# Attention and a symmetrised 7 x 7 depthwise convolution: the convolution on VectorE by even and odd parts of its kernel

## The chip, the cores and the metric

One core of a Trainium2 chip runs the whole program. The metric is the device time of one execution in microseconds (us). PE is TensorE's matmul unit, PEld its weight load, DVE is VectorE, ACT is ScalarE, POOL is GpSimd and SP is SyncE, which here only issues DMAs. Line numbers such as L524 are those of the kernel before.

## What is computed

The input x is (16, 384, 32, 32) in float32. Two residual layers follow each other, each on a group norm without affine terms (32 groups of 12 channels):

```python
x = x + attention(gn(x), w_qkv, w_proj, b_proj)   # 8 heads of 48, 1024 tokens
w_sym = (w + rot90(w, 1) + rot90(w, 2) + rot90(w, 3)) * 0.25
x = x + depthwise_conv(gn(x), w_sym, padding=3)   # 384 channels, 7 x 7
```

w_sym is unchanged by a rotation of 90 degrees, so it is also unchanged by one of 180: w_sym[dy, dx] = w_sym[-dy, -dx].

## The kernel before

**Tiles.** An image is three tiles of 128 channels by 1024 tokens (NK = 3). The 16 images go one after the other through the attention; the second norm and the convolution of image b run beside the attention of image b + 1.

**TensorE** per image: q and k for all heads (qk_step, L445), v (v_step, L471), then 64 pairs of steps: s_step (L516) makes scores of 1024 columns in PSUM, ScalarE takes their exponential (L524), av_step (L536) multiplies by v. The PSUM pool ps_s has 3 buffers, so a score step waits for the exponential of three steps before. A pair of heads ends with take (L549), sums_out (L556, L560: the softmax sums travel by SP's DMA queue), invert (L566 reciprocal, L568 and L571 the inverses out and back over SP's queue) and divide (L578). project (proj_step, L597, L605) adds the projection to x by an accumulating DMA on POOL's queue (L612). The projection of the last image is done in parts (L627, L641).

**The second norm** of image b: means on VectorE (x1_means, L1099), three squares with sums on ScalarE (x1_squares, L288), the sums gathered over groups by two DMAs on POOL's queue (ch_x L294, gs_x L296), bn_aggr (L300), then groups_x1: Ln and Exp on ScalarE (L306, L307, with two table loads), a product (L308), and spread: gr_x (L277) and sc_x (L281), two small DMAs on POOL's queue that bring scale and offset to the channels. x1_chains then has ScalarE make the normalised tiles xn (L367), one per channel tile. Image 14 takes groups_x1_vector instead, with 1/sigma on VectorE, and its x1_chains is due at once.

**The convolution.** Three of the 48 tiles run on TensorE at the very end: (14, 2), (15, 2), (15, 1), written (image, tile). Their normalised rows are stored by SP (conv_store, L758), loaded in shifted form as sh (conv_load, L765, four DMAs for a quarter of a tile), and multiplied by diagonal matrices (conv_on_pe, L799), 14 taps per half, or 13 for (14, 2). The other 45 tiles run on VectorE: conv_tap (L683) multiplies a shifted view of xn by a weight and adds it to x, once for each of 49 taps; the three tiles of an image take turns. Of (14, 0), (15, 0) and (14, 2) the seven or three taps with dx = 0 are ScalarE products (product, L664) that POOL's queue adds (add_rows, L997); (15, 0) has two sums that are added at the end (L970, L976, stores L977).

The statistics of the first norm are taken for images 2 to 15 at the start (xs, L383, L390). A general version of the whole program follows under a condition that these inputs don't meet (run(True)); it is not executed.

**The order of the work** is written out by a planner in Python, ahead of the run. clock follows TensorE, vclock VectorE. catch_up fills VectorE: what after() put into the heap later and is due comes first, then tap(), the next convolution pass. Work for ScalarE waits in applies, first in first out, with a due time and a cost; act_slot puts it between the exponentials where the cost fits a slot (3.0 us at a v step, 4.3 us between steps). Each engine and each DMA queue issues in the order that results, and an instruction that waits holds up everything behind it on its engine or queue. qk_rest issues six DMAs on POOL's queue (L461) for the q and k of an image, and begin_x the three loads of the next image's x (L164, 512 KB each). loads(1) issues one quarter of sh; in the last image it is called at the steps r = 32, 40 and 48 and at the start of the last projection.

Of the kernel before, what the change touches and what calls it, by code (L numbers as in the profile page):

```python
# [45 lines left out]
def kernel(  # L46
# [51 lines left out]
    wc = consts.tile([P, NK, KS, KS], F32, name="wc")  # L98
    nc.gpsimd.dma_start(
# [11 lines left out]

    def run(general):
        tag = "g" if general else "f"
        with ExitStack() as stack:
# [9 lines left out]
            npool = pool("npool", 6)  # L124
            qkpool = pool("qkpool", 5)
# [18 lines left out]
            LONE = (B - 1, 0)  # L144

            ROWS_ONLY = {PE_TILES[0]: (1, 2, 3), LONE: range(-PAD, PAD + 1)}

            BESIDE = None if general else (B - 2, 0)
            ROWS_ONLY[BESIDE] = range(-PAD, PAD + 1)

            def taps_of(b, k):
                return [t for t in TAPS if t[1] or t[0] not in ROWS_ONLY.get((b, k), ())]
# [49 lines left out]
            eye = wpool.tile([P, P // 4], F32, name="eye")  # L202
            wsh = wpool.tile([P, 2, 4, 2, KS], F32, name="wsh")
# [32 lines left out]
            class Stats:  # L236
# [65 lines left out]
                def groups_x1(self):  # L302

                    af = small.tile([GROUPS, 2], F32, tag="af", name=f"af_{self.name}")
                    ln = small.tile([GROUPS, 1], F32, tag="ln", name=f"ln_{self.name}")
                    nc.scalar.activation(ln, self.mv[:, 1:2], AF.Ln, bias=eps[0:GROUPS])  # L306
                    nc.scalar.activation(af[:, 0:1], ln, AF.Exp, scale=-0.5)  # L307
                    nc.scalar.activation(  # L308
                        af[:, 1:2], self.mv[:, 0:1], AF.Identity, scale=af[:, 0:1]
                    )  # L310
                    self.spread(af)

# [66 lines left out]
            def stream_in(b, k):  # L379
                if not many:  # L380
                    many["bs"] = npool.tile([P, B - 2, NK, 12], F32, tag="xn1", name="bs_all")
                many[b, k] = rpool.tile([P, N], F32, tag="x1", name=f"xs_{b}_{k}")
                nc.gpsimd.dma_start(  # L383
                    many[b, k], x[b, k * P : (k + 1) * P].rearrange("p h w -> p (h w)")
                )
# [12 lines left out]
            def stream_gather():  # L398
# [9 lines left out]
                gs = npool.tile([P, 4, PER * 12], F32, tag="xn1", name="gs_all")  # L408
# [247 lines left out]
            spare = {}  # L656

            def new_xn1(b, k):
                return npool.tile([P, N], F32, tag="xn1", name=f"xn1_{b}_{k}")

            def product(dst, b, k, dy):

                rows, src = ((slice(i.start * W, i.stop * W)) for i in region(dy)[0])
                nc.scalar.activation(  # L664
                    dst[:, rows],
                    xn1s[b, k][:, src],
                    AF.Identity,
                    scale=wsym[:, k, dy + PAD, PAD : PAD + 1],
                )
                return dst[:, rows], rows  # L670

# [3 lines left out]
            def conv_begin(st, b, k, engine):  # L675
                xn1s[b, k] = spare.pop((b, k), None) or new_xn1(b, k)
                st.apply(xn1s[b, k], x1s[b, k], k, engine)

            def conv_tap(b, k, dy, dx, dst=None):
                (oy, iy), (ox, ix) = region(dy, dx)  # L680
                dst = x1s[b, k] if dst is None else dst
                acc = dst.rearrange("p (h w) -> p h w", w=W)[:, oy, ox]
                nc.vector.scalar_tensor_tensor(  # L683
                    acc,
                    xn1s[b, k].rearrange("p (h w) -> p h w", w=W)[:, iy, ix],
                    wsym[:, k, dy + PAD, dx + PAD : dx + PAD + 1],
                    acc,
                    ALU.mult,
                    ALU.add,
                )  # L690
# [88 lines left out]
            def pe_taps(b, k):  # L779
                return [t for t in PE_TAPS if t != (1, 0) or (b, k) not in ROWS_ONLY]  # L780

            def conv_on_pe(b, k, h, first, last):
# [9 lines left out]
                taps = pe_taps(b, k)  # L792
# [120 lines left out]
            clock, vclock, last_image, catching = 0.0, 0.0, 1e9, False  # L913
            later, count = [], 0
            chains, active = deque(), []
# [14 lines left out]
            def us_tap(dy, dx):  # L930
                late_us = 0.02 if clock > last_image else 0.0
                return ((H - abs(dy)) * (W - abs(dx)) + (128 if active else 268)) / 955 + late_us

            def tap():

                while len(active) < NK and chains:
                    active.append([*chains.popleft(), 0])
                if not active:
                    return 0.0
                b, k, n = active[0]  # L940
                if (b, k) == LONE:
                    active.append(active.pop(0))
                    return tap_of_two(b, k, active[-1])
                taps = taps_of(b, k)
                c = active.pop(0)
                c[2] += 1
                if n < len(taps):
                    took = us_tap(*taps[n])
                    conv_tap(b, k, *taps[n])
                else:  # L950
                    assert not applies
                    took = us_tap(0, 0)
                    nc.vector.tensor_tensor(x1s[b, k], x1s[b, k], late["beside"], ALU.add)
                if c[2] < len(taps) + ((b, k) == BESIDE):
                    active.append(c)
                else:
                    conv_end(b, k)
                return took

            def tap_of_two(b, k, c):  # L960

                n = c[2]
                c[2] += 1
                taps = taps_of(b, k)
                if n < len(taps):
                    conv_tap(b, k, *taps[n], late["sum2"] if n % 2 else None)
                elif n == len(taps):
                    assert not adds
                    dst = late["sum2"]
                    nc.vector.tensor_tensor(dst, dst, late["sum3"], ALU.add)  # L970
                else:

                    for h in range(2):
                        cols = slice(h * HALF, (h + 1) * HALF)
                        dst = x1s[b, k][:, cols]
                        nc.vector.tensor_tensor(dst, dst, late["sum2"][:, cols], ALU.add)  # L976
                        (nc.sync, nc.scalar)[h].dma_start(  # L977
                            out[b, k * P : (k + 1) * P].rearrange("p h w -> p (h w)")[:, cols], dst
                        )
                    active.remove(c)  # L980
                return (950 + 128) / 955


            adds = deque()

            def add_step(due):
                nonlocal count
                add_rows(*adds.popleft())
                if adds:
                    due += 8.0  # L990
                    count += 1
                    heapq.heappush(later, (due, count, 0.0, lambda: add_step(due)))

            def add_rows(b, k, t, rows):
                dst = {LONE: late.get("sum3"), BESIDE: late.get("beside")}.get((b, k))
                dst = dst if dst is not None else x1s[b, k]
                nc.gpsimd.dma_start(dst[:, rows], t, accum_op=ALU.add)  # L997

            def rows_early(b, k, n, dy):
                if (b, k) == BESIDE and dy == 0:  # L1000
                    product(late["beside"], b, k, dy)
                    return

                t, rows = product(spare[B - 1, 1 + n % 2], b, k, dy)
                add_rows(b, k, t, rows)

            def lone_sums(b, k):

                product(late["sum2"], b, k, 0)
                product(late["sum3"], b, k, 1)  # L1010

            def lone_rows(b, k):

                for dy in (-1, 2, -2, 3, -3):
                    e = epool.tile([P, 2, HALF], F32, tag="e", name=f"tap_{dy}")
                    adds.append((b, k, *product(flat(e), b, k, dy)))
                add_step(now())
# [28 lines left out]
            def issue(c):  # L1046
# [15 lines left out]
                else:  # L1062
                    act_slot(3.0)
# [4 lines left out]

            applies = deque()
            ON_VECTOR = ()  # L1070

            def project(b):
                nonlocal clock
                for o in range(NK):
                    proj_step(b, o)
                    clock += US_PROJ
                    if b in ON_VECTOR:
                        after(8.0, 1.3, lambda o=o: x1_part(b, o))
                if b not in ON_VECTOR:
                    after(1.6, 0.2, lambda: x1_means(b))  # L1080

            def x1_part(b, k):

                if k == 0:
                    x1_stats[b] = Stats(f"x1_{b}")
                st = x1_stats[b]
                st.channels(x1s[b, k], k)
                if k == NK - 1:
# [431 lines left out]
```

## Time and profile before

| | us |
|---|---|
| median of 3 runs | 2910.88 (2908.89 to 2915.01) |
| the profiled execution | 2910.56 |
| its span | 2908.8 |
| mean granted TensorE clock | 0.991 of full speed |
| VectorE in L683, 2170 taps | 2362.5 |
| ScalarE in L524, 1024 exponentials | 1020.4 |
| TensorE in L516 and L536 | 1037.8 and 1036.8 |

The span runs from the first to the last record of the profiled execution; the execution's own time lies 1.76 us above it. A share of busy time is a mean over the span. In a timeline, a row gives the start, the time, the engine and line, the operation, its output and inputs, how many instructions were joined in the row, and in brackets how long the engine sat idle before it and what ended that. A list of waits gives, for an engine and line, what it waited for, the total, the number of times and the longest. A row of windows gives busy time and instruction count for PE, PEld, DVE, ACT and POOL in turn, then the granted clock, the busy share of the DMA engines and GB/s.

### The profile page before, as it was taken

Reading aid. Unit: us, or ns where it says so; the run is one execution under the profiler, and the core shown is the slowest. Engines: PE = TensorE matmul, PEld = TensorE weight load, DVE = VectorE, ACT = ScalarE, POOL = GpSimd, SP = SyncE. Lnnn points to the kernel's source line nnn. Section 1 sums busy time; section 2 is a strip of 40 time slices with the busy share of each in tenths; the row PEclk is TensorE's granted clock in tenths of the full one; section 3 lists DMA queues with packets and bytes.
Section 4 is the critical chain, followed back from the end, with each engine's and each line's share of the span. In section 5 each row is a group of like instructions: output and inputs, shape, how many; then the busy total and the mean of one; then the engine's idle time right before and its main releaser. Section 6 shows DMA issues by size and latency. Waiting matters only on the chain. (4 is left out here: it accounts for less than half of the span.)

```text
span 2908.8 us, 46868 instructions
## 1 busy us (share of the span) xinstructions
PE 2860.4 (98%) x19638; PEld 1137.1 (39%) x19638; DVE 2570.7 (88%) x2562; ACT 1573.6 (54%) x1873; POOL 252.2 (9%) x411
## 2 busy tenths in 40 slices
PE   9999999999999999999999999999999999998986
PEld 5343343433434343443434334343443434343332
DVE  4502999999999999999999999999999999999679
ACT  3637556374754737466473745637375473744720
POOL 3200012000101001010100101000010100101100
PEclk9999999999999999999999999999999999999998
DMA  6621121121302122121212212122131212212625
GB/s 239 184 44 41 28 57 50 38 70 25 81 20 65 38 43 63 29 70 33 65 38 42 64 29 55 46 42 64 29 77 27 58 39 42 64 29 43 154 58 149
DMA packets 77485, 176.86 MB, mean 61 GB/s; under 512 B 32096, under 2 KB 34032, under 8 KB 75728
## 3 DMA queue, kind: packets, MB, share of 16 engines
q0 software_dynamic: 34336, 114.90, 15.6%
q1 hardware_dynamic: 41216, 55.21, 7.3%
q10 hardware_dynamic: 1712, 3.67, 0.4%
q8 instruction: 156, 2.56, 0.4%
q14 instruction: 65, 0.53, 0.1%
HBM read 118.61 MB, written 28.72 MB: 51 GB/s over the span
## 5 line engine op out<-in xcount | busy, mean ns | idle before, releaser
L683 DVE SCALAR_TENSOR_TENSOR x<-xn,wsym,x 128x930 f32<-128x930 f32 (+9 forms) x2170 | 2362.5, 1162 | 14.7 <-ACT xn L367 14.7
L524 ACT ACTIVATE e<-ps_s 128x1024 f32<-128x1024 f32 x1024 | 1020.4, 1029 | 484.0 <-PE ps_s L516 483.4
L516 PE MATMUL ps_s<-qk 48*64 48x512 f32 x8192 | 1037.8, 590 | 11.7 <-ACT e L524 11.7
L536 PE MATMUL acc<-e,v 64*64 64x512 f32 x8192 | 1036.8, 590 | 0.0
L516 PEld LDWEIGHTS ps_s<-qk 48*64 48x64 f32 x8192 | 309.0, 133 | 588.4 <-issue 534.6
L536 PEld LDWEIGHTS acc<-e,v 64*64 64x64 f32 x8192 | 311.4, 133 | 571.7 <-issue 570.8
L445 PE MATMUL ps_qk<-x,wqk 128*128 128x512 f32 x1152 | 502.4, 595 | 0.0
L445 PEld LDWEIGHTS ps_qk<-x,wqk 128*128 128x128 f32 x1152 | 218.1, 190 | 277.7 <-issue 269.3
L452 ACT COPY qk<-ps_qk 128x1024 f32<-128x1024 f32 x96 | 97.2, 1013 | 333.9 <-PE ps_qk L445 333.5
L471 PE MATMUL ps_v<-wv,x 128*128 128x384 f32 x768 | 252.6, 486 | 0.0
L597 PE MATMUL ps_proj<-o,wp 128*128 128x512 f32 x540 | 234.2, 592 | 0.0
L491 ACT COPY v<-ps_v 64x384 f32<-64x384 f32 x256 | 121.6, 475 | 150.8 <-PE ps_v L471 148.5
L471 PEld LDWEIGHTS ps_v<-wv,x 128*128 128x128 f32 x768 | 145.9, 190 | 108.2 <-issue 14.4
L612 POOL DMA_DIRECT2D x<-in_x x45 | 39.3, 874 | 1610.8 <-ACT x L605 1439.0
L597 PEld LDWEIGHTS ps_proj<-o,wp 128*128 128x128 f32 x540 | 102.6, 190 | 126.2 <-issue 122.2
L566 DVE RECIPROCAL rec<-sums 128x16 f32<-128x16 f32 x63 | 15.6, 248 | 152.2 <-DMA sums<-sum 152.2
L605 ACT ACTIVATE x<-ps_proj,bp 128x1024 f32<-128x1024 f32 x45 | 50.2, 1115 | 167.5 <-PE ps_proj L597 167.5
L578 DVE TENSOR_TENSOR o<-o,inv 128x1024 f32<-128x1024 f32 x63 | 76.8, 1218 | 48.2 <-DMA inv<-inv 36.4
L549 ACT COPY o<-acc 128x512 f32<-128x512 f32 x128 | 68.5, 591 | 72.0 <-PE acc L536 72.0
L390 DVE BATCH_NORM_STATS2 bs_all<-xs 128x6 f32<-128x512 f32 x84 | 52.7, 681 | 39.6 <-DMA xs<-in_x 39.5
L799 PE MATMUL ps_conv<-sh,mat 128*32 128x480 f32 (+3 forms) x656 | 68.0, 569 | 0.0
L367 ACT ACTIVATE xn<-x,sc_x 128x1024 f32<-128x1024 f32 x47 | 55.3, 1271 | 11.6 <-DVE sc_x L357 7.2
(144 smaller groups left out, 594.8 us busy)
## 6 DMA issues: line engine op xcount, KB each, us to landing
x<-in_x POOLq DMA_DIRECT2D x90, 512.0 KB, 5.6
inv<-inv SPq DMA_DIRECT2D x126, 256.0 KB
out<-x POOLq DMA_DIRECT2D x45, 512.0 KB, 3.7
xs<-in_x POOLq DMA_DIRECT2D x42, 512.0 KB, 6.9
qk<-qk POOLq DMA_DIRECT2D x96, 128.0 KB, 4.2
o<-o SPq DMA_DIRECT2D x180, 32.0 KB
sh<-xd SPq DMA_DIRECT2D x32, 160.0 KB
x<-in_x SPq DMA_DIRECT2D x6, 512.0 KB
```

The source lines that it names most:

```text
L445: nc.tensor.matmul(ps[:, h, :], lhsT=wqk[:, k, s, t, :], rhs=xns[b][:, k, h * HALF : (h + 1) * HALF], start=(k == 0), stop=(k == NK - 1),)
L452: nc.scalar.copy(halves(qks[u][:, s, :]), ps)
L471: nc.tensor.matmul(ps[:, j, 0:C], lhsT=xns[b][:, k, t * P : (t + 1) * P], rhs=wv[:, k, :], start=(k == 0), stop=(k == NK - 1),)
L491: nc.scalar.copy(dst[:, :, 0 : HEADS // 2 * (D + 1)].rearrange("p k (h d) -> p k h d", d=D + 1)[:, :, :, 0:D], src.rearrange("p k (h d) -> ...
L516: nc.tensor.matmul(ps[64 * c : 64 * c + 64, a, :], lhsT=qk[r, 1, 64 * kb : 64 * kb + 64], rhs=qk[r, 0, h * HALF : (h + 1) * HALF], start=True,
L524: nc.scalar.activation(es[n], ps, AF.Exp, scale=SCALE)
L536: nc.tensor.matmul(accs[a][64 * j : 64 * j + 64, :], lhsT=v[rows, kb, c : c + 64], rhs=e[rows, j, :], start=(kb == 0), stop=(kb == 2 * NT ...
L549: nc.scalar.copy(half_of(w)[:, a, :], accs.pop(a))
L578: nc.vector.tensor_tensor(o, o, invs.pop(u).rearrange("p (a n) -> p a n", a=2), ALU.mult)
L597: nc.tensor.matmul(ps[:, h, :], lhsT=wp[:, t, o * P : (o + 1) * P], rhs=os_[b, t // 2][:, t % 2, h * HALF : (h + 1) * HALF], start=(t == 0 ...
L683: nc.vector.scalar_tensor_tensor(acc, xn1s[b, k].rearrange("p (h w) -> p h w", w=W)[:, iy, ix], wsym[:, k, dy + PAD, dx + PAD : dx + PAD + 1],
L799: nc.tensor.matmul(dst[CH * i : CH * (i + 1), :].rearrange("p (y x) -> p y x", x=W)[:, :, ox], lhsT=mats[k][:, i, d0 * KS + dx + PAD, :], ...
```

## The change

**The passes.** With w_sym[dy, dx] = w_sym[-dy, -dx], the kernel is split by dx: even(dy, dx) is half the sum and odd(dy, dx) half the difference of w_sym at dx and -dx (four more small VectorE operations at the start; odd vanishes for dx = 0 and for dy = 0). For each tile ScalarE writes the normalised rows into a padded tile with a pitch of 35 (fold_x) and makes the three products with even(dy, 0), dy = 1 to 3 (fold_first). VectorE makes three sums and three differences of the view shifted by +dx and -dx (side), builds three rows of sums with even and three with odd weights, and adds each to the output shifted by +dy and by -dy, with the sign turned for the odd ones. That makes 34 passes and three products by tensor_scalar for each tile instead of 49 taps, one tile at a time.

**ScalarE** no longer makes products of single tap rows (L664, with L970, L976 and L997), and Ln and Exp of the second norm are gone: all images take groups_x1_vector. The three squares of the norm may stand at a v step, since the slot there is 4.3 instead of 3.0. applies becomes a heap by due time. x1_chains of every image is due 9 us after the statistics, that of image 14 too. prepare decides when fold_x and fold_first of a tile are put into applies.

**Order and buffers.** On POOL's queue gr_x and sc_x of an image stand directly behind the three loads of L164; ch_x and gs_x stand before the six DMAs of L461. npool has named tiles in one buffer instead of six rotating ones, qkpool 4 buffers instead of 5; the matrix tile mat_1 lies in the space of wqk and the masks in that of wv. loads(1) is called at r = 32 and 40 only. All three TensorE tiles have 14 taps per half. The last tile on VectorE is (15, 0), whose last addition is cut in two halves with a store each.

```diff
+        near, far = wsym[:, :, PAD:, PAD:], wsym[:, :, PAD:, PAD::-1]
+        nc.vector.tensor_tensor(even, near, far, ALU.add)
+        nc.vector.tensor_scalar(even, even, 0.5, None, ALU.mult)
+        nc.vector.tensor_tensor(odd, near, far, ALU.subtract)
+        nc.vector.tensor_scalar(odd, odd, 0.5, None, ALU.mult)
...
-            npool = pool("npool", 6)
-            qkpool = pool("qkpool", 5)
+            npool = pool("npool", 6 if general else 1)
+            qkpool = pool("qkpool", 4)
...
-            LONE = (B - 1, 0)
-
-            ROWS_ONLY = {PE_TILES[0]: (1, 2, 3), LONE: range(-PAD, PAD + 1)}
-
-            BESIDE = None if general else (B - 2, 0)
-            ROWS_ONLY[BESIDE] = range(-PAD, PAD + 1)
-
-            def taps_of(b, k):
-                return [t for t in TAPS if t[1] or t[0] not in ROWS_ONLY.get((b, k), ())]
+            LAST = (B - 1, 0)
...
+                padded = [
+                    npool.tile([P, H * PITCH + 2 * PAD], F32, name=f"padded_{i}") for i in range(2)
+                ]
+                for t in padded:
+                    nc.gpsimd.memset(t, 0.0)
+                sides = [npool.tile([P, N], F32, name=f"side_{j}") for j in range(PAD)]
+                rows_e = [npool.tile([P, N], F32, name=f"rows_e{i}") for i in range(PAD)]
...
-                def groups_x1(self):
-
-                    af = small.tile([GROUPS, 2], F32, tag="af", name=f"af_{self.name}")
-                    ln = small.tile([GROUPS, 1], F32, tag="ln", name=f"ln_{self.name}")
-                    nc.scalar.activation(ln, self.mv[:, 1:2], AF.Ln, bias=eps[0:GROUPS])
-                    nc.scalar.activation(af[:, 0:1], ln, AF.Exp, scale=-0.5)
-                    nc.scalar.activation(
-                        af[:, 1:2], self.mv[:, 0:1], AF.Identity, scale=af[:, 0:1]
-                    )
-                    self.spread(af)
...
+            def padded_view(i, d=0):
+
+                return padded[i % 2][:, PAD + d : PAD + d + H * PITCH].rearrange(
+                    "p (h w) -> p h w", w=PITCH
+                )[:, :, 0:W]
+
+            def fold_x(i, st, b, k):
+                nc.scalar.activation(
+                    padded_view(i),
+                    grid(x1s[b, k]),
+                    AF.Identity,
+                    bias=st.sc[:, k, 1:2],
+                    scale=st.sc[:, k, 0:1],
+                )
+
+            def fold_first(i, k):
+
+                for dy in range(1, PAD + 1):
+                    nc.scalar.activation(
+                        grid(rows_e[dy - 1]),
+                        padded_view(i),
+                        AF.Identity,
+                        scale=even[:, k, dy, 0:1],
+                    )
...
+                def side(j, n, op):
+                    vec.tensor_tensor(grid(sides[n]), padded_view(i, j), padded_view(i, -j), op)
+
+                def into(dst, src, w):
+                    vec.scalar_tensor_tensor(dst, src, w, dst, ALU.mult, ALU.add)
+
+                def first(dst, src, w):
+                    vec.tensor_scalar(dst, src, w, None, ALU.mult)
+
+                def shifted(src, dy, op, half=None):
+                    lo, hi = max(0, -dy) * W, (H - max(0, dy)) * W
+                    if half is not None:
+                        lo, hi = (lo, N // 2) if half == 0 else (N // 2, hi)
+                    dst = out_t[:, lo:hi]
+                    vec.tensor_tensor(dst, dst, src[:, lo + dy * W : hi + dy * W], op)
...
+                for j in (1, 2, 3):
+                    sums.append((full, lambda j=j: side(j, j - 1, ALU.add)))
+                outs.append((full, lambda: into(grid(out_t), padded_view(i), e(0, 0))))
+                for j in (1, 2, 3):
+                    outs.append((full, lambda j=j: into(out_t, sides[j - 1], e(0, j))))
+
+                def out_rows(t, dy, second):
+                    part = ((H - dy) * W + 128) / 955
+                    outs.append((part, lambda: shifted(t(), dy, ALU.add)))
+                    outs.append((part, lambda: shifted(t(), -dy, second)))
+
+                for dy in (1, 2, 3):
+                    for j in (1, 2, 3):
+                        sums.append(
+                            (full, lambda dy=dy, j=j: into(rows_e[dy - 1], sides[j - 1], e(dy, j)))
+                        )
+                    out_rows(lambda dy=dy: rows_e[dy - 1], dy, ALU.add)
+                for n, j in enumerate((2, 3, 1)):
+                    sums.append((full, lambda j=j, n=n: side(j, n, ALU.subtract)))
+                slot = {2: 0, 3: 1, 1: 2}
+                for n, (dy, (j, l)) in enumerate(((1, (2, 3)), (2, (3, 1)), (3, (1, 2)))):
+                    sums.append(
+                        (ts, lambda dy=dy, j=j, n=n: first(rows_o[n % 2], sides[slot[j]], o(dy, j)))
+                    )
+                    sums.append(
+                        (full, lambda dy=dy, l=l, n=n: into(rows_o[n % 2], sides[slot[l]], o(dy, l)))
+                    )
+                    out_rows(lambda n=n: rows_o[n % 2], dy, ALU.subtract)
...
+            applies, count_a = [], 0
+
+            def add_apply(when, cost, f):
+
+                nonlocal count_a
+                count_a += 1
+                heapq.heappush(applies, (when, count_a, cost, f))
...
+            def prepare():
+
+                n = state["x"]
+                if n < len(order) and n < state["done"] + 2:
+                    state["x"] += 1
+                    add_apply(now() + (1.0 if n > state["done"] else 0.0), 1.3, lambda n=n: prepare_x(n))
+                n = state["rows"]
+                if n < len(order) and n <= state["free"] and n in ready_x:
+                    state["rows"] += 1
+                    add_apply(now() + (2.5 if n > state["done"] else 0.0), 3.6, lambda n=n: prepare_rows(n))
+
+            def prepare_x(n):
+                b, k, st = order[n]
+                fold_x(n, st, b, k)
+                ready_x[n] = now() + 2.0
+                prepare()
+
+            def prepare_rows(n):
+                fold_first(n, order[n][1])
+                ready_rows[n] = now() + 4.0
+                prepare()
...
-                    act_slot(3.0)
+                    act_slot(4.3)
...
-                after(11.0, 3.3 if b == B - 2 else 0.6, lambda: x1_aggregate(b, st))
+                after(11.0, 3.3, lambda: x1_aggregate(b, st))
 
             def x1_aggregate(b, st):
                 st.aggregate()
-                if b == B - 2:
-
-                    st.groups_x1_vector()
-                    applies.append((now(), 3.7, lambda: x1_chains(b, st)))
-                else:
-                    applies.append((now() + 0.5, 0.6, lambda: x1_groups(b, st)))
-
-            def x1_groups(b, st):
-                st.groups_x1()
-                applies.append((clock + 9.0, 3.7, lambda: x1_chains(b, st)))
+                st.groups_x1_vector()
+                add_apply(now() + 9.0, 1.3, lambda: x1_chains(b, st))
...
+                order.extend((b, k, st) for k in range(NK) if (b, k) not in on_pe)
+                prepare()
...
-                if b == B - 1 and r in (32, 40, 48):
+                if b == B - 1 and r in (32, 40):
```

## Prediction

> **What bounds the kernel now.** I read the busy shares first, then what TensorE waited for, then each wait's neighbourhood in the timelines, then the end. The page:
>
> ```profile
> span 2908.8 us, 46868 instructions
> ## 1 busy us (share of the span) xinstructions
> PE 2860.4 (98%) x19638; PEld 1137.1 (39%) x19638; DVE 2570.7 (88%) x2562; ACT 1573.6 (54%) x1873; POOL 252.2 (9%) x411
> ```
>
> TensorE is busy for 98% of the span; VectorE's 88% lies beside it. So work saved on VectorE is worth only the time in which TensorE waited, plus the tail after TensorE's last instruction. The list of TensorE's waits is short:
>
> ```profile
> PE ps_s L516 <- ACT e L524: 11.7, 2, 7.8
> PE ps_proj_last L641 <- DVE o L578: 8.7, 1, 8.7
> PE ps_proj_last L641 <- DVE o L627: 1.5, 1, 1.5
> ```
>
> The columns are total us, times, longest. All of it falls after 2660 us, in the last two images. The ScalarE timeline tells what stood behind the two waits for an exponential:
>
> ```profile
> 2661.18 3.50 ACT L367 ACTIVATE xn<-x,sc_x 128x1024 f32<-128x1024 f32 x3 [4.36 <-DMA sc_x<-gr_x]
> ...
> 2686.80 1.12 ACT L664 ACTIVATE xn<-xn,wsym 128x992 f32<-128x992 f32 x1 [10.64 <-DVE x L683]
> ```
>
> ScalarE stood 4.36 us for the second norm's scales of image 14, and 10.64 us for a buffer that VectorE's taps still read; TensorE needs the exponential of three steps back (ps_s has 3 buffers), so it lost 3.89 and 7.80 us. It then ran slow:
>
> ```profile
> 2665.64 1.99 PE L516 MATMUL ps_s<-qk 48*64 48x512 f32 x8 [3.89 <-ACT e L524]
> ...
> 2672.32 1.03 PE L516 MATMUL ps_s<-qk 48*64 48x512 f32 x8
> ```
>
> Eight such matmuls take 1.99 us at 2665.64 and 1.03 us at 2672.32; the granted clock between is 0.50. That costs 3.24 us more; after the 7.80 wait it costs 1.86.
>
> **The stalls that go.** (1) and (2): image 14's chain gets the same 9 us delay as the others before ScalarE takes it up, and the products of L664 are gone: 3.89+3.24+7.80+1.86 = **16.8**. (3) The 8.7 wait for the last division, by SP's queue:
>
> ```profile
> 2711.50 0.33 SPq L568 DMA_DIRECT2D inv<-rec  x1
> 2712.92 1.16 SPq L571 DMA_DIRECT2D inv<-inv  x2
> ...
> 2772.67 1.71 SPq L765 DMA_DIRECT2D sh<-xd  x4
> 2774.48 0.37 SPq L568 DMA_DIRECT2D inv<-rec  x1
> 2777.71 1.13 SPq L571 DMA_DIRECT2D inv<-inv  x2
> ```
>
> The reciprocal was done at 2766.1, but inv<-rec sat on SP behind four sh loads that waited for a buffer. The change drops this group of loads (r = 48). The chain from issue to division took 2782.78-2774.48 = 8.3 us; from 2766.2 it ends at 2774.5, and TensorE is free for it at 2775.39: no wait, 8.67 and 2.1 of slow clock gone, less 0.4 for a chain that may be a little later: **10.4**. (4) The reciprocals of L627 came 1.54 late because taps stood between: **1.5** (no slow clock behind it, so none to gain). Sum 28.7.
>
> **The tail.** TensorE's last conv matmul starts at 2883.31; VectorE runs taps until 2902.36 and the span ends at 2908.8. With 34 passes and 3 cheap ones per tile VectorE is done before TensorE: 22 full passes at about 1.2 us (L578 and L970: 1.23 each, overlapping by some 0.1), 3 tensor_scalar at 0.81 (L363), 12 shifted adds of 928 to 992 elements at 1.10 to 1.16, sum 42.4 us, against 49 x 1.09 = 53 (2362.5 us for 2170 taps); over 45 tiles 2362 becomes some 1910. Then TensorE's end decides, and it moves later. The load sh for the third quarter of (14,2) now stands on SP behind the stores of both image-15 tiles, which follow the norm's apply at 2827.2: it lands near 2832.5 by the landing of the load issued at 2829.63, while TensorE is through with the part before at 2828.3: 4.2 us of wait, 2.5 of slow clock (between the 1.86 and 3.24 above), and two more taps for (14,2), 2 x 0.82 (46.24 us for 56 taps) = 1.65. TensorE's end 2883.9+8.35 = 2892.2, half an add 0.67, store issue and the same 4.8 us to the end: 2898.2 instead of 2908.8, **10.6** gained (13 without the slow clock, 17 without the wait). Start: two memsets of padded on POOL and four small VectorE operations lie beside the loads; taken as 0, up to 2. Gain in all 28.7+10.6 = 39.3.
>
> **What the change adds to every image.** ScalarE loses Ln, Exp, their two table loads (3.4 us) and three applies (3.5), and takes three folds (1.17 each, by L367's 1.23 and the 1.17 of its back-to-back interval) and nine row products (1.05 to 1.12 each, L664): 13 us against 7, in slots of 3.6 us between exponentials. At 54% busy it has room: each slot leaves the three-deep ps_s ring full again within some 5 steps, where it idles 0.70 us per 1.72 us step. What has no room is a wait inside ScalarE's queue. The fold needs sc_x, and sc_x now starts directly behind other work on POOL's queue:
>
> ```profile
> 1789.48 0.96 POOL L461 DMA_DIRECT2D qk<-qk  x2 [0.33 <-ACT qk L452]
> 1790.43 1.61 POOL L164 DMA_DIRECT2D x<-in_x  x3
> 1814.69 0.61 POOL L277 DMA_DIRECT2D gr_x<-af_x  x1 [22.65 <-ACT af_x L308]
> 1818.71 0.78 POOL L281 DMA_DIRECT2D sc_x<-gr_x  x1 [3.41 <-DMA gr_x<-af_x]
> ```
>
> Before, ScalarE made the scales and gr_x followed the loads of the next image by 24 us; now VectorE makes them a v-step earlier, and in the changed order gr_x and sc_x stand right behind the three loads (1.5 MB). The fold stands on ScalarE behind the eighth exponential, which ends at 1798.85. Without waiting in the queue: gr_x issued by 1792.05+0.61 = 1792.66, +3.41, +0.78, +2.03 from sc_x's issue to ScalarE (2659.15 to 2661.18) = 1798.88: no stall at all. If its packets wait for the loads': SP's rows above show such a case. inv<-rec alone was followed after 1.08 us (2711.83 to 2712.92), behind four loads of 160 KB after 2.86 (2774.85 to 2777.71): the small transfer waited for what was ahead on its queue. When do the loads end? Image by image the windows differ; the one whose qk transfers were out of the way, as the earlier squares make them in the changed order, issued its loads at 1963.95:
>
> ```profile
> 1970.00:1970.50 0.50, 0.50 (x12) 0.16 (x7) 0.50 (x1) 0.40 (x1) 0.00 (x0) 1.00 0.14 57
> 1970.50:1971.00 0.50, 0.50 (x8) 0.15 (x4) 0.50 (x2) 0.50 (x1) 0.00 (x0) 1.00 0.00 0
> ```
>
> Last column GB/s: the flow ends 6.5 us after the issue; in the image at 1790.43 it ends 8.8 us after (41 GB/s at 1798 to 1799, 4 at 1799 to 1800). With 6.5: 1796.9, +0.25 for gr_x's own packets, +2.46 from them to sc_x's issue (1816.25 to 1818.71), +0.78, +2.03 = **1802.4**. Following the steps by hand (exponential 0.93 in a run, step 1.72, S needs the exponential of three back; the same count gives 4.15 for the 3.89 measured), TensorE loses nothing up to 1799.7 and 1 us per us after it: 2.7, less the count's 0.25, about 2.4 per image. Loads of L164 stand in 14 images; image 0's chain comes with six exponentials ahead instead of eight and loses 6.1 and 3 of slow clock, 9 in all; the other thirteen 13 x 2.4 = **31**. Image 14's has no loads ahead: 0.1.
>
> The ends of 2.4: 0 (not held up) and 5.0 (loads as at 1790.43). I take 2.4 because the qk transfers are away early, as in that row.
>
> A rule on the slow clock: "TensorE: Matmul & The Clock Gate" of the Trainium skill, under "What's actually happening", says that the clock halves after an idle window of about 3.4 us. The stalls of 3.89 and 7.80 agree, the 1.54 without loss too; by the page the stalls of about 1 and 1.6 us that make up the 2.4 cost no clock. A rule against the change: "SBUF — State Buffer", under "Who interferes with whom", says that VectorE's tensor_scalar can lock GpSimd out, so that its descriptors wait. No row here shows it; by it gr_x and sc_x could each be 0.8 us later, 13 x 1.6 = 21 more.
>
> From the rows alone, the clock after a stall between 1.54 (no loss) and 3.89 (3.24 lost) is open: 0 to 3.24 for each of thirteen, 0 to 42. I take 0, since the two pieces (1.06 and 1.64) are near 1.54.
>
> **Sum.** Span 2908.8-39.3+31+9+0.1 = 2909.6; what lies around the span is 1.76 (2910.56 for that execution), so **2911**. That execution stands at the median of the three runs (2910.88).
>
> **Rivals.**
> A (0.50), as above. It nearly cancels: 0.45 us per image is 0.2% (5.8 us, the bound of what counts as no change). Loads' end of 5.4 to 7.6 us: 2897 to 2926.
> B (0.22), small transfers are not held up by the loads on POOL's queue: 2908.8-39.3+1.8 = **2871**. For it: SP's case is another queue. Against: its 1.78 us.
> C (0.23), the other side: the loads last as at 1790.43. sc_x reaches ScalarE at 1802.4+2.3 = 1804.7, 5.0 per image, 65+11 for image 0: 2908.8-39.3+76+1.8 = **2947**; with the slow clock up to 2989. It decides once the loads end later than 6.4 us after their issue: from there on the loss of 13 images is more than the gain.
> D (0.05), the change doesn't make VectorE faster: if passes over the padded view (pitch 35, no row for it) take a quarter longer, a tile costs 53 us again and the tail stays: **2922**.
>
> **Numbers.** Faster: B, and 0.3 of A: 0.37. Within 0.2%: 0.4 of A: 0.20. Slower: 0.3 of A, C, D: 0.43. The range goes from B with a tail gain up to 17 (2866) to C with part of the clock loss (2955).
>
> **What would show it.** Right: TensorE's list has L516 waits on exponentials some 13 to 30 times, 1 to 3 us each, with sc_x's wait on ScalarE just before; gr_x to sc_x on POOL takes 6 to 7 us instead of 3.41; VectorE falls to some 70%; no waits at 2661, 2681 and 2775; TensorE waits some 4 us for sh before the end. Wrong: gr_x to sc_x still 3.4 (B), over 8 (C), VectorE near 85% (D), or ScalarE waiting for VectorE's buffers, which the order as I read it does not show.

## The result and the profile after

The changed kernel takes 2924.01 us (median of 7 runs, 2921.03 to 2929.47) against 2913.06 for the kernel before in the same comparison (7 runs): a ratio of 1.0041, interval 1.0029 to 1.0053. Line numbers from here on are those of the changed kernel: L517 scores, L525 exponentials, L692 fold_x, L703 row products, L913 convolution on TensorE. The page of the changed kernel:

```profile
span 2921.8 us, 46612 instructions
## 1 busy us (share of the span) xinstructions
PE 2871.4 (98%) x19654; PEld 1254.2 (43%) x19654; DVE 2076.9 (71%) x2247; ACT 1644.4 (56%) x1921; POOL 244.3 (8%) x398
```

VectorE lost 494 us of work and the span grew by 13. TensorE's list of waits:

```profile
PE ps_s L517 <- ACT e L525: 37.5, 23, 2.8
PE ps_conv L913 <- DMA sh<-xd: 4.5, 1, 4.5
```

The two long waits for an exponential, the 8.7 us for the last division and the 1.5 for the reciprocals are gone. In their place stand 23 waits of at most 2.8 us, and one for sh. POOL's queue in the image shown in the prediction:

```profile
1821.28 0.96 POOL L462 DMA_DIRECT2D qk<-qk  x2 [2.81 <-ACT qk L453]
1822.23 1.62 POOL L164 DMA_DIRECT2D x<-in_x  x3
1823.85 0.65 POOL L287 DMA_DIRECT2D gr_x<-af_x  x1
1832.01 0.79 POOL L291 DMA_DIRECT2D sc_x<-gr_x  x1 [7.52 <-DMA gr_x<-af_x]
```

sc_x could be issued 7.52 us after gr_x, where it was 3.41 before. ScalarE's timeline shows who waited:

```profile
1834.98 1.25 ACT L692 ACTIVATE padded<-x,sc_x 128x1024 f32<-128x1024 f32 x1 [4.33 <-DMA sc_x<-gr_x]
1836.14 1.91 ACT L525 ACTIVATE e<-ps_s 128x1024 f32<-128x1024 f32 x2
1837.94 3.25 ACT L703 ACTIVATE rows_e<-padded,even 128x1024 f32<-128x1024 f32 x3
```

The fold waits 4.33 us for the scales, two exponentials follow, and then three row products take 3.25 us. TensorE pays twice:

```profile
1837.19 1.09 PE L517 MATMUL ps_s<-qk 48*64 48x512 f32 x8 [1.61 <-ACT e L525]
...
1842.15 1.09 PE L517 MATMUL ps_s<-qk 48*64 48x512 f32 x8 [1.29 <-ACT e L525]
```

The list counts from a modelled end of the matmuls. So I count the whole loss by the exponentials, which both kernels do in the same number: from the first one of image 2 to the first one of image 15 the changed kernel takes 48.7 us more, **3.74 per image**. The 13 us of span are then: the first exponential of the run 1.8 earlier, image 0 4.1 longer, image 1 0.0, images 2 to 14 48.7 longer, image 15 16.5 shorter, and from the last exponential to the end 114.6 instead of 136.0, 21.4 shorter.

### The profile page after: what moved, and what is told of

It reads as the page before. It is cut to its first block, busy times and chain, and to the rows that moved or that the text cites. A ratio compares the mean times of both kernels' runs of the same rounds, so it can differ in the third digit from the quotient of the medians.

```text
span 2921.8 us, 46612 instructions
## 1 busy us (share of the span) xinstructions
PE 2871.4 (98%) x19654; PEld 1254.2 (43%) x19654; DVE 2076.9 (71%) x2247; ACT 1644.4 (56%) x1921; POOL 244.3 (8%) x398
## 4 chain that ended last, share of the span: by engine, by line
PE 90%; issue 4%; ACT 3%; DMA 2%; POOL 1%; DVE 0%; SPq 0%; POOLq 0%; ACTq 0%
PE acc L537 27%; PE ps_s L517 25%; PE ps_qk L446 17%; PE ps_v L472 8%; PE ps_proj L598 8%; PE ps_conv L913 2%; DMA sc_x<-gr_x 1%; ACT e L525 1%; ACT rows_e L703 1%; PE ps_proj_last L642 1%; POOL x L164 1%; DMA gr_x<-af_x 1%; ACT qk L453 0%; POOL qk L462 0%; PE warm L1280 0%
## 5 line engine op out<-in xcount | busy, mean ns | idle before, releaser
L525 ACT ACTIVATE e<-ps_s 128x1024 f32<-128x1024 f32 x1024 | 1016.4, 1029 | 401.1 <-PE ps_s L517 400.5
L517 PE MATMUL ps_s<-qk 48*64 48x512 f32 x8192 | 1066.1, 592 | 37.5 <-ACT e L525 37.5
L517 PEld LDWEIGHTS ps_s<-qk 48*64 48x64 f32 x8192 | 360.6, 133 | 568.7 <-issue 454.6
L537 PEld LDWEIGHTS acc<-e,v 64*64 64x64 f32 x8192 | 378.8, 133 | 508.6 <-issue 498.8
L724 DVE SCALAR_TENSOR_TENSOR rows_e<-side,even,rows_e 128x1024 f32<-128x1024 f32 x405 | 510.6, 1279 | 1.1
L721 DVE TENSOR_TENSOR side<-padded 128x1024 f32<-128x1024 f32 x270 | 329.8, 1221 | 247.2 <-ACT padded L692 247.2
L734 DVE TENSOR_TENSOR x<-x,rows_o 128x992 f32<-128x992 f32 (+3 forms) x271 | 311.0, 1148 | 3.0
L734 DVE TENSOR_TENSOR x<-x,rows_e 128x992 f32<-128x992 f32 (+2 forms) x270 | 310.2, 1149 | 0.0
L724 DVE SCALAR_TENSOR_TENSOR rows_o<-side,odd,rows_o 128x1024 f32<-128x1024 f32 x135 | 172.9, 1281 | 1.6
L724 DVE SCALAR_TENSOR_TENSOR x<-side,even,x 128x1024 f32<-128x1024 f32 x135 | 172.7, 1280 | 0.0
L703 ACT ACTIVATE rows_e<-padded,even 128x1024 f32<-128x1024 f32 x135 | 146.8, 1164 | 0.0
```

The lines of the kernel that those rows point to most:

```text
L517: nc.tensor.matmul(ps[64 * c : 64 * c + 64, a, :], lhsT=qk[r, 1, 64 * kb : 64 * kb + 64], rhs=qk[r, 0, h * HALF : (h + 1) * HALF], start=True,
L525: nc.scalar.activation(es[n], ps, AF.Exp, scale=SCALE)
L537: nc.tensor.matmul(accs[a][64 * j : 64 * j + 64, :], lhsT=v[rows, kb, c : c + 64], rhs=e[rows, j, :], start=(kb == 0), stop=(kb == 2 * NT ...
L703: nc.scalar.activation(grid(rows_e[dy - 1]), padded_view(i), AF.Identity, scale=even[:, k, dy, 0:1],)
L721: vec.tensor_tensor(grid(sides[n]), padded_view(i, j), padded_view(i, -j), op)
L724: vec.scalar_tensor_tensor(dst, src, w, dst, ALU.mult, ALU.add)
```

## The experiments

My theory, called Q: gr_x waits behind the loads on POOL's queue, and the wait stands in ScalarE's queue. Rival T: the DMA engines are busy with the loads, whatever the queue. Rival S: ScalarE's new slot overruns by itself. The first three runs move the same transfers to other places.

**Loads on SP.**

```diff
-                queue = nc.gpsimd if b > 1 else nc.sync
+                queue = nc.sync
```

> The changed kernel, with the three loads of the next image's x issued on SP's queue instead of POOL's; nothing else differs, and the order on TensorE, VectorE and ScalarE is the same. In the changed kernel each of images 2 to 14 loses 3.74 us (48.7 in all) where the fold waits for the second norm's scales. Theory Q (gr_x waits behind the loads on POOL's queue): from gr_x's end to sc_x takes 3.4 to 4.0 us instead of 7.5, TensorE's waits for an exponential of 1.3 to 2.8 us in images 2 to 14 are gone, and the time is 2924 - 48.7 = 2875 us, within 5. Rival T (the DMA engines are simply busy with the loads, whatever the queue): gr_x to sc_x stays at 6 to 8 us and the time above 2910. Rival S (ScalarE's new slot is too long: a fold of 1.25 us and three row products of 3.25 with two exponentials between them overrun the three score buffers by themselves): the second wait of 1.3 us (1.84 with its surroundings) stays in 13 images, and the time is about 2924 - 48.7 + 24 = 2899.

Measured: 2916.9 us, ratio to the kernel before 1.0012 (1.0003 to 1.0022). SP issued the three loads at 1813.93. POOL's queue:

```profile
1815.23 0.96 POOL L462 DMA_DIRECT2D qk<-qk  x2 [4.55 <-ACT qk L453]
1816.18 0.65 POOL L287 DMA_DIRECT2D gr_x<-af_x  x1
1825.23 0.80 POOL L291 DMA_DIRECT2D sc_x<-gr_x  x1 [8.40 <-DMA gr_x<-af_x]
```

No load stands on this queue any more, and the small transfer took 8.40 us. As a rule of queue order alone, Q falls. The loss per image is 3.36 us, a little less than in the changed kernel; gr_x itself is issued earlier there, 1.20 us after the image's first exponential instead of 2.81.

**Small transfers on SP.**

```diff
-                    nc.gpsimd.dma_start(
+                    (nc.sync if self.name[:2] == "x1" else nc.gpsimd).dma_start(
                         gr_d, af.unsqueeze(1).to_broadcast([GROUPS, PER, 2])
...
-                    nc.gpsimd.dma_start(
+                    (nc.sync if self.name[:2] == "x1" else nc.gpsimd).dma_start(
                         self.sc, gr_d.rearrange("g e s -> (g e) s").rearrange("(k p) s -> p k s", p=P)
```

> The changed kernel, with the two small transfers gr_x and sc_x of the second norm on SP's queue; the loads stay on POOL's queue and flow at the same time as before. Theory Q: gr_x to sc_x takes at most 4 us, no waits in images 2 to 14, 2875 us within 5. Rival T (busy DMA engines): the small packets share the engines with the same loads at the same moment, so gr_x to sc_x takes 6 us or more, and at least half of the 48.7 us stays: over 2899. Rival S: as for the run with the loads on SP's queue, 2899.

Measured: 2880.69 us, ratio 0.9881 (0.9864 to 0.9897). The time is what Q gave, but for another reason: on SP gr_x no longer had to wait for POOL's earlier issues, so it was issued at 1797.18, ahead of the loads (1799.57), and was done in 3.43. sc_x came after them, alone on its queue:

```profile
1797.18 0.59 SPq L287 DMA_DIRECT2D gr_x<-af_x  x1
1801.20 0.38 SPq L291 DMA_DIRECT2D sc_x<-gr_x  x1
```

Between 1801.6 and 1806.0 the DMA view (packets, MB, share of the 16 engines by queue) has nothing of SP's queue (q1):

```profile
DMA packets 287, 1.05 MB, mean 239 GB/s; under 512 B 33, under 2 KB 33, under 8 KB 284
## 3 DMA queue, kind: packets, MB, share of 16 engines
q0 software_dynamic: 287, 1.05, 74.6%
```

Its packets ran between 1806.0 and 1809.0, when the loads were nearly through, and the fold began at 1809.55, 7.97 us after sc_x's issue (2.18 in the changed kernel; the first row is the DMA view of 1806.0 to 1809.0):

```profile
q1 hardware_dynamic: 400, 0.00, 7.9%
1809.55 1.26 ACT L692 ACTIVATE padded<-x,sc_x 128x1024 f32<-128x1024 f32 x1 [1.58 <-DMA sc_x<-gr_x]
```

So T holds in one form: the small transfer waited for the flow of the loads though it was alone on its queue. That busy engines alone hold it up is not shown, since their share was only 0.16 from 1801.6 to 1802.6. It cost little here, 0.47 us per image, because gr_x had gone ahead; T's own forecast for this run, over 2899, took gr_x to be held up as well.

**Loads behind the small transfers.**

```diff
-                            begin_x(b + 1)
+                            after(6.0, 0.0, lambda: begin_x(b + 1))
```

> The changed kernel, with the loads of the next image due 6 us later, so that gr_x and sc_x stand ahead of them on POOL's queue. Theory Q: gr_x to sc_x 3.4 us, no waits in images 2 to 14, 2875 us within 5; the loads start some 5 to 6 us later and are still done 15 us before their norm is applied. Rival T: the same here, as the loads haven't begun. Rival S: 1.84 us stay in 13 images, 2899. Rival L (the loads were late enough already): TensorE waits for the next image's x or its scales, above 2890.

Measured: 2877.56 us, ratio 0.9882 (0.9866 to 0.9899).

```profile
1791.07 0.61 POOL L287 DMA_DIRECT2D gr_x<-af_x  x1 [0.26 <-issue]
1796.57 0.80 POOL L291 DMA_DIRECT2D sc_x<-gr_x  x1 [4.88 <-DMA gr_x<-af_x]
```

With only the two qk transfers ahead it takes 4.88 us; the run with the loads on SP had the same two ahead on this queue and took 8.40, so the loads added 3.5 from the other queue. The loss is 0.12 us per image: S falls, since the fold and the three row products stand in the same order, and rival L too. The 3.4 us that Q had for gr_x to sc_x did not come, though its time did.

**1/sigma on ScalarE again.**

```diff
-                st.groups_x1_vector()
-                add_apply(now() + 9.0, 1.3, lambda: x1_chains(b, st))
+                if b == B - 2:
+                    st.groups_x1_vector()
+                    add_apply(now() + 9.0, 1.3, lambda: x1_chains(b, st))
+                else:
+                    add_apply(now() + 0.5, 0.6, lambda: x1_groups(b, st))
...
+            def x1_groups(b, st):
+                st.groups_x1()
+                add_apply(clock + 9.0, 1.3, lambda: x1_chains(b, st))
```

> The changed kernel, with one part undone: 1/sigma of the second norm by Ln and Exp on ScalarE again, for all images but image 14, as in the kernel before; POOL's queue still has gr_x directly behind the loads in its order. ScalarE then works out the scales behind the fifth exponential, and the first fold stands behind the fifteenth instead of the eighth. Theory Q: gr_x is issued some 8 us or more after the loads, its way to sc_x takes 3.4 to 4.5 us, and the fold finds its scales there; the two table loads and three small operations (3.4 us) fit the slot as they did before. 2875 us within 6. Rival S (the fold and the row products overrun by themselves, and ScalarE has 3.4 us more to do): at least 1.84 us per image stay, 2899 or more.

Measured: 2907.87 us, ratio 0.9982 (0.9972 to 0.9991). gr_x to sc_x is 3.54 (median of 13 images) and no wait for an exponential is left, but another took its place. The time is in S's range, and S's wait, for an exponential, is not there: with the fold seven exponentials later, the copies of the attention's output come late (L548 and L561 are av_step and take in this run).

```profile
PE acc L548 <- ACT o L561: 23.1, 15, 3.2
```

That costs 2.25 us per image.

**One exponential more ahead of the fold.**

```diff
-                add_apply(now() + 9.0, 1.3, lambda: x1_chains(b, st))
+                add_apply(now() + 11.0, 1.3, lambda: x1_chains(b, st))
```

> The changed kernel, with the chain of the second norm due 11 us after the statistics instead of 9; the first fold then stands behind nine exponentials instead of eight, 1.72 us later, in the same queue. The scales themselves come as late as before. Theory (the loss is a wait inside ScalarE's queue: TensorE loses what the scales come later than a limit that the place of the fold sets): the limit moves by one step, so each of 13 images loses about 3.74 - 1.72 = 2.0 us, 22 us less in all: 2902, within 6. Rival (the scales are late because ScalarE or VectorE asks for them so, and move with the fold): no change, 2924. Rival S (ScalarE's copies of the attention's output, three exponentials after the last slot, become late instead): a new wait of TensorE for acc, above 2915.

Measured: 2895.01 us, ratio 0.9944 (0.9927 to 0.9960). gr_x to sc_x stays at 7.41, and the loss falls to 1.67 us per image, 2.07 less where I had 1.72; the time is 1 us beyond my margin, on the good side. So the place of the fold in ScalarE's queue sets the limit, and both rivals fall.

**One load ahead instead of three.**

```diff
-                load_x(b)
+                load_x(b, (0,))
+                after(6.0, 0.0, lambda: load_x(b, (1, 2)))
```

> The changed kernel, with one of the three loads of x ahead of gr_x on POOL's queue and the other two due 6 us later, behind sc_x: 512 KB ahead of the small transfer instead of 1.5 MB. In the changed kernel gr_x to sc_x takes 7.5 us with three loads ahead, and 4.9 with none in the run with the loads behind. Theory (the small transfer is done when the flow ahead of it is done, and 1 MB takes some 3 us of the 5 us flow of 1824.0 to 1829.3): 4.5 to 5.2 us, and with at least 2.5 us less the loss of 3.74 per image falls to 0.5 to 1.2: 2882 to 2892. Rival (any load in flight costs the small transfer the whole delay, as of a fixed latency): 7 us or more, above 2910.

Measured: 2889.54 us, ratio 0.9927 (0.9910 to 0.9943): in the range, with a delay of 5.89 instead of 4.5 to 5.2 and a loss of 1.18. So the delay grows with what flows ahead:

| kernel | ahead of gr_x | gr_x to sc_x, median of 13 images, us | loss per image, us |
|---|---|---|---|
| loads behind | qk | 5.06 | 0.12 |
| one load ahead | qk, 512 KB | 5.89 | 1.18 |
| one exponential more | qk, 1.5 MB | 7.41 | 1.67 |
| changed kernel | qk, 1.5 MB | 7.54 | 3.74 |
| loads on SP | qk, and 1.5 MB on another queue | 8.43 | 3.36 |

**The tail's load**, on top of the loads behind.

```diff
                     first_half(b)
-                    loads(1)
+                    loads(2)
```

> The run with the loads behind the small transfers (2877.56 us), with one more edit: two quarters of sh are loaded at the start of the last projection instead of one, so that the fourth quarter of (14, 2) no longer stands on SP behind the stores of image 15's tiles. There TensorE waited 4.57 us for it, and the 104 matmuls after it took 12.50 us where 224 later ones took 23.07, so 1.8 us of slow clock. My theory of the tail (TensorE's end sets the end of the span, VectorE is done 13 us before it): the wait goes and the time falls by 4.57 + 0.2 + 1.8 = 6.5 us, to about 2871. Rival (the end is set by VectorE, as in the kernel before): no change, 2877.

Measured: 2867.17 us, ratio 0.9841 (0.9826 to 0.9855), against 2877.56: 10 us, more than the 6.5 of the wait and its slow clock (the profiled spans differ by 3.3; from the last exponential to the end it takes 7.5 less, but image 0 is 4.4 longer here, for a reason left open). The wait for sh is gone from TensorE's list. This version beats both kernels.

**VectorE's saving taken back**, on top of that.

```diff
-                    sums.append((full, lambda j=j: side(j, j - 1, ALU.add)))
+                    sums.append((four, lambda j=j: [side(j, j - 1, ALU.add) for _ in range(4)]))
```

> The same kernel as the run with the tail's load moved, but with VectorE's saving taken back by hand: each of the three sums of a tile is made four times over (the same values written again), nine more passes of about 1.17 us per tile, so that a tile costs 42.4 + 10.5 = 53 us as 49 taps did, and VectorE is busy for 89% again. Theory (TensorE bounds; what VectorE saves is worth only the tail): the time stays within 3 us of that run but for the last tiles, where VectorE has 13 us in hand and is asked for 10.5 to 20 more, so 0 to +10 us. Rival (VectorE's speed is what gained the 35 us between the kernel before and the repaired one): the time goes back to 2905 to 2913.

Measured: 2900.2 us, ratio 0.9954 (0.9939 to 0.9968): 33 us more than without the extra passes, neither my 0 to 10 nor the rival's whole. In its profile the last exponential comes 9 us later, and the stretch from there to the end takes 132.0 instead of 105.9 us: VectorE adds until 2897.2, after TensorE is done. Images 2 to 4 lose 8.7 us more than without the extra passes, with a wait of 1.4 to 1.6 us in each for ScalarE's copies of the attention's output; in images 5 to 14 TensorE covers the passes. I had mis-sized the tail: from the last exponential until its last pass VectorE is busy for 116.4 us instead of 65.1, as it gets there a whole tile late. The run is not the same order otherwise: the planner counts the extra passes and puts the fold later, in image 10 behind 13 exponentials instead of eight.

**Two parts alone, in the kernel before** (with its line numbers). Image 14's chain later:

```diff
-                    applies.append((now(), 3.7, lambda: x1_chains(b, st)))
+                    applies.append((now() + 9.0, 3.7, lambda: x1_chains(b, st)))
```

> The kernel before with one part of the change: the second norm's chain of image 14 is due 9 us after the statistics, instead of at once. Theory (the stall of 3.89 us at 2661 and its slow clock of 3.24 come from ScalarE standing for the scales): both go, 2912.8 - 7.1 = 2905.7. Rival (the row products that follow move with it and find their buffers even less free, or VectorE starts image 14's tiles later and ends later): the time falls by less than 3 us or rises.

Measured: 2903.61 against 2912.39 us, ratio 0.9967 (0.9954 to 0.9980): 8.8 us less, as the theory had it (7.1) within the interval; of the two waits for exponentials one of 7.4 us is left.

One group of loads less:

```diff
-                if b == B - 1 and r in (32, 40, 48):
+                if b == B - 1 and r in (32, 40):
```

> The kernel before with one part of the change: loads of sh at r = 32 and 40 only. Theory (the last division waited 8.67 us for inverses that sat on SP behind the four loads of r = 48): the wait at 2775 and 2.1 us of slow clock are gone. As VectorE, which sets the end here, waited 11.24 us for the same inverses, the whole 10.4 us show in the time if the taps move up with it: 2902.4. If VectorE has taps to run in that gap that it would have had to run anyway, only a part shows. Rival (another wait takes the place, because the loads then stand later in the same queue): a change of less than 3 us.

Measured: 2921.11 us, ratio 1.0031 (1.0019 to 1.0044), 9 us slower, against theory and rival. The division's wait is gone, but:

```profile
PE ps_conv L799 <- DMA sh<-xd: 17.3, 2, 10.6
PE ps_s L516 <- ACT e L524: 12.3, 2, 8.1
```

Two quarters of sh came late (6.64 and 10.63 us), and VectorE, which sets the end there, stood for a result that TensorE makes behind each of them:

```profile
2840.22 0.15 DVE L1302 TENSOR_REDUCE good<-ps_again 1x1 f32<-1x2 f32 x1 [8.64 <-PE ps_conv L799]
2899.19 0.69 DVE L820 TENSOR_TENSOR x<-ps_conv,x 128x512 f32<-128x512 f32 x1 [11.61 <-PE ps_conv L799]
```

In the kernel before it stood 11.24 us for the division instead. The rival had the right kind, a wait in the place of the one removed, and too small a size. In the changed kernel VectorE no longer sets the end; what the same edit is worth there by itself no run shows.

## Why the prediction was right, and where it was not

- **The near balance and its place in the time line** were right: case A, 2911 with 2897 to 2926 as its own range, and 2924 measured. The gains at the old waits and in the tail cancel against a wait of every fold for its scales. The sum gave no sign, 2911 against 2910.88; the kernel is slower by 0.41%, which had the largest of the three chances (0.43).
- **Stalls (1) and (2)**: 16.8 forecast, 16.5 measured in image 15. **(3), (4) and the tail**: 22.5 forecast, 21.4 measured. The wait for sh was 4.52 us for 4.2. As a sum these hold; (3) alone does not carry over to the kernel before, as the last run shows.
- **The loss per image** is the term that was mis-sized: 2.4 forecast, 3.74 measured, 17.5 us over 13 images, more than the whole error. gr_x to sc_x took 7.54 where the sum had 6.95 (1792.66 to 1799.61) and the sign of being right 6 to 7. The reason is the end of the loads: I took 6.5 us after their issue, from one image of the kernel before; in the changed kernel, issued at 1822.23, they flow for some 7.1:

```profile
1828.50:1829.00 0.50, 0.50 (x12) 0.20 (x8) 0.00 (x0) 0.43 (x1) 0.00 (x0) 1.00 0.78 282
1829.00:1829.50 0.50, 0.50 (x12) 0.22 (x8) 0.00 (x0) 0.00 (x0) 0.00 (x0) 1.00 0.09 27
1829.50:1830.00 0.50, 0.50 (x12) 0.18 (x8) 0.00 (x0) 0.38 (x1) 0.00 (x0) 1.00 0.00 0
```

The fold began 2.18 instead of 2.03 after the issue, and the 0.25 that I took off for the count by hand should have stayed: the list shows each wait about 0.25 too short (1.61 and 1.29 in image 10, where 3.42 were lost). With the slow clock below, some 0.2 on the mean, that makes about 1.2 of the 1.34 that 2.4 falls short of 3.74.
- **Image 0's 9 us** failed as a step: there the loads were issued at 244.41, after gr_x (236.22) and sc_x (240.75), and image 1 lost nothing. I had given it the place of the others. Image 0 itself lost 4.1 us, between 145 and 164 us, which I had not. It was luck that this term was 4.9 too high and that the first exponential came 1.8 earlier, for which I had no term: together they hide 6.7 of the 17.5 us.
- **The reason for the wait** was argued from one queue, and that part is wrong. I had split A from B by whether POOL's queue holds small transfers behind the loads. The runs show that the flow of the loads holds them on another queue as well (8.43 us and 7.97 us); SP's inv<-rec, which I cited, fits both. A repair by another queue for the loads, which my reason would have offered, gained 7 of 46 us. The other reason that I cited, VectorE's tensor_scalar against POOL's descriptors, no run isolates; with the same VectorE passes and the loads behind, the loss is 0.12 us per image, so little is left for it.
- **D and C**: VectorE fell to 71% (70 forecast), so the passes cost nearly what the rows said. C's loads to 8.8 us did not come; its slow clock came in part.
- **The slow clock** I took as 0 for these stalls. It halved in five of the thirteen images, after waits of 1.75 to 2.80 us. The windows of the changed kernel behind the wait of 2.07 us at 957.55 (third number from the right: granted clock):

```profile
959.00:960.00 1.00, 1.00 (x12) 0.32 (x8) 1.00 (x2) 1.00 (x2) 0.00 (x0) 0.53 0.00 0
960.00:962.00 2.00, 2.00 (x12) 0.54 (x8) 2.00 (x3) 2.00 (x3) 0.00 (x0) 0.50 0.00 0
```

In these images the second wait vanishes, as TensorE's slower steps let ScalarE catch up: they lose 4.03 us on the mean, the other eight 3.57. So it cost about 0.5 us where it came, not 3.24. Waits of 2.05 and 2.10 in two other images left the clock at 1.00, so the length of the wait alone does not decide it. The page "TensorE: Matmul & The Clock Gate" of the Trainium skill, under "What's actually happening", has the clock halve after an idle window of about 3.4 us; here it halved after listed waits of 1.75 us, about 2.0 in full, and the measurement decides.

## What to carry to other kernels

When a change lets a small transfer be issued earlier, look for the bulk transfers that then flow at the same time, on all queues: here 4 us of delay in a 3 KB transfer, once per image, ate all that the change had gained with 494 us less work on VectorE. Put the small one ahead of the bulk; another queue alone does not free it. Here 6 us of a due time brought 46 us. And a part that removes a wait is worth what is late next: one load left out, worked out at 10.4 us of gain, lost 9 us in the kernel before.

## What I had not expected of the hardware

A transfer alone on its queue had no packet for 4.4 us while another queue moved 287. The page "DMA: Bandwidth & Descriptors" of the Trainium skill says, under "Queues, rings and completion order", that each DMA engine takes turns between queues packet by packet; by that one would expect sc_x's packets among those of the loads, and this run does not show it. Whether its descriptors or its data were held up stays open.

From its first exponential to that of image 1, image 0 took 0.5 us (one exponential more) to 7.5 us (1/sigma on ScalarE) longer than in the kernel before; two runs with the same order on TensorE and ScalarE, the changed kernel and the loads on SP, differ by 2.2. No run here settles why.
